# Per-tile waits on reused memory, and an adjacency proof that shares its stage with the next layer's prologue

## The chip, the cores and the metric

The kernel runs on one core of a Trainium2 chip. The metric is the time of one execution on the device in microseconds (us); three runs of the kernel before give a median of 2050.09 us. The engines are TensorE (PE, its weight loads PEld), VectorE (DVE), ScalarE (ACT), GpSimd (POOL) and SyncE (SP). SP and POOL here mostly issue transfers (DMA); "SPq" or "ACTq" in a view means that engine's queue of instructions.

## What is computed

Four graph layers run over 4096 nodes with 128 features and one dense adjacency matrix of 4096 x 4096 (f32, symmetric in the inputs, ones at about 1.6% of the places). Each layer's result is added to its input and normalised per row:

```python
x = _layernorm(x + _L0_gnn_ref(x, adj, ...))   # hyperbolic attention over pairs
x = _layernorm(x + _L1_gnn_ref(x, adj, ...))   # 4-head transformer attention
x = _layernorm(x + _L2_gnn_ref(x, adj, ...))   # normalised graph convolution
x = _layernorm(x + _L3_gnn_ref(x, adj, ...))   # additive attention, masked softmax
```

The part of layer 1 that the change touches is

```python
q = x @ Wq + bq;  k = x @ Wk + bk;  v = x @ Wv + bv        # 4 heads of 32
attn = einsum('nhc,mhc->hnm', q, k) / sqrt(32)
e = where(adj == 0, 0, exp(attn - rowmax));  out = (e / sum(e)) @ v
x_r = x @ Ws + bs                                            # gated with out
```

## The kernel before, in words

The adjacency is tiled in 8 x 8 blocks of 512 x 512. A class `Fast` computes everything under assumptions on the data (symmetric adjacency of zeros and ones, bounded scores) and proves them on the way; if a proof fails, a general class `Net` computes all again. With these inputs only `Fast` does work.

The program is written in a tile framework. Code opens pools (`tc.tile_pool`), which are laid out one above the other as a stack in SBUF or in the eight banks of PSUM, and takes tiles from them; a closed pool's memory is given to the next one. The framework inserts the semaphores. It also plans, at compile time, one fixed order of instructions for each engine, by priority (earlier code first) among what its own simulated clock says is ready; on the chip each engine works through its list in order. Inside `tc.manual_schedule()` the written order is kept, but other instructions can be placed between.

The stages, with times from the profile:

- **Layer 0** (0 to about 721 us). A short prologue, then `pair_loop` (L1709; to 646) over the 36 block pairs I <= J, in an order written out by hand (`SHARED_ORDER`). Its pools are `sg0`, `wk0` and PSUM pools `ps_z0`, `ps_i0`, `ps_j0`, all eight banks. Beside it POOL copies the adjacency as bf16 into the DRAM tensor `adjb` (`narrow`, L1917, last issued at 544). The end of layer 0 (L510 to L602 and `normalise_tile`) works on all 32 row tiles of X and finishes with ACT L232, in eight groups of four tiles.
- **The proof of symmetry**, `mirror` (L1664), is called at L513, between the pair loop and the end of layer 0. For each block pair SP loads `low` (L1683) and `up` (L1686), 512 KB each, into three buffers each (pool `mirt`); PE adds the block, weighted by -2^k, and the transposed mirror block, weighted by 2^k, into a PSUM bank (L1692, L1697; pool `mirp`, two banks); after twelve quarter blocks DVE takes the largest absolute value into a column of `odd` (L1702). There are 28 pairs, then 8 diagonal blocks: 64 loads, 144 quarter blocks, 12 reductions.
- **Layer 1's prologue**, in `layer1` (L2150), from the `with ExitStack() as pctx` on. PE transposes X into `XT` in eight groups (L163 in a helper; copies L178 on ACT, L180 on DVE). Then for each of eight column chunks and for k and q: a projection on PE (L2201), its rounded part by ACT (L2203) and its rest by DVE (L2204) into a tile `cut` (512 KB), a maximum by DVE (L2207), and a transfer to the DRAM tensor `qk` by SP (L2210). For the first two chunks POOL reads `qk` back as stacks of heads into `KS` and `QS` (`stack`, L2181, four transfers of 256 KB each time). Then V (PE L2216, DVE L2217) and the residual projection R (PE L2226, DVE L2227; R is the tile `Y` of later stages). All PSUM tiles of this stage come from the pool `ps_t`, eight banks, one bank each, in rotation. The last step is `good` (L2241).
- **Attention**, `attention_unshifted` (L1941), 789.9 to 1589.8: 256 steps of scores (PE L1994), exponential (ACT L2001), mask (DVE L2003) and weighted sum (PE L2020), two steps apart. `ps_s` takes six banks, `ps_v` two. Each output block has an `ending`.
- **Layers 2 and 3**, `layers23` (L2245): `Y` is split into three bf16 parts (`split`, ACT L2353, DVE L2355), PE convolves with blocks in a `ring` (L2372), and DVE looks at rows of the adjacency in tiles `nat` (loads L2331, L2336). Then `attend_factored` (L1573).

The pools that a stage opens wait, before their first use, for every earlier user of each pool on whose memory they lie.

Of the kernel before, what the change touches and what calls it, by code (L numbers as in the profile page):

```python
# [9 lines left out]
F32 = mybir.dt.float32  # L10
F32R = mybir.dt.float32r
# [6 lines left out]
P = 128  # L18
# [43 lines left out]
class Net:  # L62
# [30 lines left out]

    def copies(self):
        self.adjT = self.dram.tile([self.NS, self.NS, P, 4, S], F32, tag="adjT", name="adjT")

    def pools(self, ctx, adj, big, t, o):

        self.on_scalar = 4
        if adj:  # L100
            self.adjp = ctx.enter_context(self.tc.tile_pool(name="adjp", bufs=adj))
        if big:
            self.ps_big = ctx.enter_context(self.tc.tile_pool(name="ps_big", bufs=big, space=PSUM))
        self.ps_t = ctx.enter_context(self.tc.tile_pool(name="ps_t", bufs=t, space=PSUM))
        self.ps_o = ctx.enter_context(self.tc.tile_pool(name="ps_o", bufs=o, space=PSUM))
# [202 lines left out]
    def layer0(self, x, weight, bias, att_w, att_b):  # L308
# [4 lines left out]
        with ExitStack() as ctx:  # L313
            self.on_scalar = 4
            keep = ctx.enter_context(tc.tile_pool(name="keep0", bufs=1))
            self.cols = ctx.enter_context(tc.tile_pool(name="cols0", bufs=1))
            adp = ctx.enter_context(tc.tile_pool(name="ad0", bufs=2))
            pre_pools = ctx.enter_context(ExitStack())
            pre = pre_pools.enter_context(tc.tile_pool(name="pre0", bufs=2))
            self.ps_t = pre_pools.enter_context(tc.tile_pool(name="ps_t", bufs=6, space=PSUM))  # L320
            one = pre_pools.enter_context(tc.tile_pool(name="one0", bufs=1))
            self.wide = pre_pools.enter_context(tc.tile_pool(name="wide", bufs=1))
            ps_c = pre_pools.enter_context(tc.tile_pool(name="ps_c", bufs=1, space=PSUM))
# [187 lines left out]
            late = ctx.enter_context(tc.tile_pool(name="late0", bufs=1))  # L511
            rot = ctx.enter_context(tc.tile_pool(name="rot0", bufs=6))
# [92 lines left out]
    def pair_loop(self, HT, HA, dr, rows, adp, early, rows4):  # L605
# [7 lines left out]
        with ExitStack() as ctx:  # L613
            atp = ctx.enter_context(tc.tile_pool(name="at0", bufs=2))
            wtp = ctx.enter_context(tc.tile_pool(name="sg0", bufs=6))
            wk = ctx.enter_context(tc.tile_pool(name="wk0", bufs=2))
            ps_t = ctx.enter_context(tc.tile_pool(name="ps_t0", bufs=2, space=PSUM))
            ps_z = ctx.enter_context(tc.tile_pool(name="ps_z0", bufs=2, space=PSUM))
            ps_i = ctx.enter_context(tc.tile_pool(name="ps_i0", bufs=1, space=PSUM))
            ps_j = ctx.enter_context(tc.tile_pool(name="ps_j0", bufs=1, space=PSUM))  # L620
# [224 lines left out]
    def layer1(self, Wq, bq, Wk, bk, Wv, bv, Ws, bs, Wb, R):  # L845
# [6 lines left out]
        with ExitStack() as ctx:  # L852
            self.on_scalar = 4
            keep = ctx.enter_context(tc.tile_pool(name="keep1", bufs=1))
# [27 lines left out]
            with ExitStack() as pctx:  # L882
                pre = pctx.enter_context(tc.tile_pool(name="pre1", bufs=1))
                rot = pctx.enter_context(tc.tile_pool(name="rot1", bufs=2))
                self.ps_t = pctx.enter_context(tc.tile_pool(name="ps_t", bufs=8, space=PSUM))
# [59 lines left out]
    def attention_unshifted(self, VA, KS, QS, at0, stack, R, wb):  # L945
# [4 lines left out]
        with ExitStack() as ctx:  # L950
            rot = ctx.enter_context(tc.tile_pool(name="rotf", bufs=1))
            natp = ctx.enter_context(tc.tile_pool(name="natf", bufs=2))
            atp = ctx.enter_context(tc.tile_pool(name="atf", bufs=1))
            ep = ctx.enter_context(tc.tile_pool(name="ef", bufs=3))
            ps_s = ctx.enter_context(tc.tile_pool(name="ps_s", bufs=3, space=PSUM))
            ps_v = ctx.enter_context(tc.tile_pool(name="ps_v", bufs=1, space=PSUM))
# [198 lines left out]
    def attention_shifted(self, V, qk, R, wb, spare):  # L1155
# [4 lines left out]
        with ExitStack() as ctx:  # L1160
            self.pools(ctx, 1, 2, 3, 1)
            self.wide = ctx.enter_context(tc.tile_pool(name="wide", bufs=2))
            keep = ctx.enter_context(tc.tile_pool(name="keeps", bufs=1))
            self.cols = ctx.enter_context(tc.tile_pool(name="cols1", bufs=1))
# [12 lines left out]
            work = ctx.enter_context(tc.tile_pool(name="work1", bufs=1))  # L1177
# [98 lines left out]
    def layers23(self, w2, weight, bias, a_s, a_r, out, Y):  # L1276
# [6 lines left out]
        with ExitStack() as ctx:  # L1283
            RING = 8
            ring = ctx.enter_context(tc.tile_pool(name="ring", bufs=1)).tile([P, RING, 4, S], F32, tag="ring", name="ring")
            keep = ctx.enter_context(tc.tile_pool(name="keep3", bufs=1))
# [10 lines left out]
            pre = pctx.enter_context(tc.tile_pool(name="pre3", bufs=1))  # L1297
            rot = pctx.enter_context(tc.tile_pool(name="rot2", bufs=2))
            wp = pctx.enter_context(tc.tile_pool(name="w2", bufs=4))
            ps_b = pctx.enter_context(tc.tile_pool(name="ps_b", bufs=2, space=PSUM))  # L1300
            ps_t = pctx.enter_context(tc.tile_pool(name="ps_t", bufs=2, space=PSUM))
            ps_s = pctx.enter_context(tc.tile_pool(name="ps_s", bufs=2, space=PSUM))
            ps_a = pctx.enter_context(tc.tile_pool(name="ps_a", bufs=2, space=PSUM))
# [228 lines left out]
    def attend_factored(self, F, XB, rho, col, wx, tot, eps, a0, ring, out):  # L1532
        nc, tc, N, NT, NS, D, X = self.nc, self.tc, self.N, self.NT, self.NS, self.D, self.X
        with ExitStack() as ctx:
            rot = ctx.enter_context(tc.tile_pool(name="rot3", bufs=2))
            RING = ring.shape[1]
            wp = ctx.enter_context(tc.tile_pool(name="w3", bufs=4))
            ps_a = ctx.enter_context(tc.tile_pool(name="ps_a3", bufs=2, space=PSUM))
            ps_b = ctx.enter_context(tc.tile_pool(name="ps_b3", bufs=2, space=PSUM))
# [43 lines left out]
    def attend(self, H, Rb, ring, weight, br, a_s, a_r, out):  # L1583
        nc, tc, N, NT, D, X = self.nc, self.tc, self.N, self.NT, self.D, self.X
        with ExitStack() as ctx:
            self.pools(ctx, 0, 0, 6, 2)
            self.wide = ctx.enter_context(tc.tile_pool(name="wide", bufs=2))
            one = ctx.enter_context(tc.tile_pool(name="one3", bufs=1))
            self.cols = ctx.enter_context(tc.tile_pool(name="cols3", bufs=1))
# [4 lines left out]
            with tc.tile_pool(name="pre3", bufs=1) as pre:  # L1594
# [15 lines left out]
            work = ctx.enter_context(tc.tile_pool(name="work3", bufs=1))  # L1610
# [33 lines left out]
class Fast(Net):  # L1644

    MARKS = 112

# [16 lines left out]
    def mirror(self, ctx):  # L1664
# [3 lines left out]
        keep = ctx.enter_context(tc.tile_pool(name="mir", bufs=1))  # L1668
        rot = ctx.enter_context(tc.tile_pool(name="mirt", bufs=3))
        ps = ctx.enter_context(tc.tile_pool(name="mirp", bufs=2, space=PSUM))  # L1670
# [38 lines left out]
    def pair_loop(self, HT, HA, dr, rows, adp, early, rows4):  # L1709
# [7 lines left out]
        with ExitStack() as ctx:  # L1717
            wtp = ctx.enter_context(tc.tile_pool(name="sg0", bufs=6))
            wk = ctx.enter_context(tc.tile_pool(name="wk0", bufs=2))
            ps_z = ctx.enter_context(tc.tile_pool(name="ps_z0", bufs=4, space=PSUM))  # L1720
            ps_i = ctx.enter_context(tc.tile_pool(name="ps_i0", bufs=1, space=PSUM))
            ps_j = ctx.enter_context(tc.tile_pool(name="ps_j0", bufs=1, space=PSUM))
# [218 lines left out]
    def attention_unshifted(self, VA, KS, QS, at0, stack, R, wb):  # L1941
# [3 lines left out]
        W = C + 1  # L1945
        with ExitStack() as ctx:
            rot = ctx.enter_context(tc.tile_pool(name="rotf", bufs=1))
            natp = ctx.enter_context(tc.tile_pool(name="natf", bufs=2))
            atp = ctx.enter_context(tc.tile_pool(name="atf", bufs=1))
            ep = ctx.enter_context(tc.tile_pool(name="ef", bufs=3))  # L1950
            ps_s = ctx.enter_context(tc.tile_pool(name="ps_s", bufs=3, space=PSUM))
# [627 lines left out]
```

## Time and profile before

| what | value |
|---|---|
| median of three runs | 2050.09 us (2048.27 to 2053.14) |
| the profiled execution | 2050.21 us, span 2048.4 us, mean granted PE clock 0.954 |
| PE busy | 1900.9 us, 93% of the span |
| DVE busy | 1736.6 us, 85% |
| ACT busy | 1328.8 us, 65% |
| POOL busy | 171.4 us, 8% |
| moved by DMA | 350.22 MB, mean 171 GB/s |
| pair loop | about 76 to 646 us |
| end of layer 0 | 646 to 721 us |
| proof | first load 646.0, last reduction 744.8 us |
| layer 1's prologue | 745.7 to 789.8 us |
| attention | 789.9 to 1589.8 us |

A row of the page's groups names line, engine and operation, the tile written and those read, count, busy time and mean, and the idle time of the engine just before with what ended it. A row of the waits reads "who <- whom: us in total, times, longest us". A row of the chain gives start, length and what ran or was waited for; the chain is followed back from the last instruction. A row of the windows gives, for one stretch, the busy us of each engine with instruction counts in brackets, then the granted clock, the mean busy share of the DMA engines, and what they moved. Matmul ends are modelled, and DMA shares can come out above 1.

### The profile page before, as it was taken

How to read it: one execution, taken by the hardware profiler on the slowest of the kernel's cores; microseconds unless marked ns; L12 is line 12 of the kernel's file. 1: busy time of each engine (PE TensorE's matmuls, PEld its weight loads, DVE VectorE, ACT ScalarE, POOL GpSimd, SP SyncE). 2: the span in 40 equal slices, each digit the busy share in tenths (PEclk: the TensorE clock that was granted, in tenths of full speed). 3: DMA queues.
4: the chain of work that ended last, by engine and by line, in shares of the span. 5: the costliest groups of instructions: out<-in, count | busy, mean ns of one | idle time of the engine just before them, and what ended most of it. 6: DMA issues, size and time to landing. Idle time of an engine off the chain costs nothing.

```text
span 2048.4 us, 23818 instructions
## 1 busy us (share of the span) xinstructions
PE 1900.9 (93%) x8648; PEld 978.9 (48%) x8680; DVE 1736.6 (85%) x2685; ACT 1328.8 (65%) x1681; POOL 171.4 (8%) x269
## 2 busy tenths in 40 slices
PE   4789999999997788999999999999999799999997
PEld 4257766666666454333333333333333344444443
DVE  6579999998988946789999999999999777778986
ACT  5589999999997723777787777778787322210000
POOL 2211112111100221300000000000000000000000
PEclk8569999999999998999999999999999999999999
DMA  3488989899825977853535453545343799934441
GB/s 101 49 139 147 155 167 157 155 163 168 144 93 191 363 277 223 199 152 132 144 124 146 136 150 134 144 133 155 124 139 118 290 396 373 340 116 156 155 148 43
DMA packets 138064, 350.22 MB, mean 171 GB/s; under 512 B 13196, under 2 KB 56364, under 8 KB 125648
## 3 DMA queue, kind: packets, MB, share of 16 engines
q1 hardware_dynamic: 82944, 230.27, 32.3%
q0 software_dynamic: 45632, 50.69, 20.1%
q10 hardware_dynamic: 9360, 67.64, 9.9%
q8 instruction: 70, 1.15, 0.2%
q14 instruction: 58, 0.48, 0.1%
HBM read 371.54 MB, written 44.12 MB: 203 GB/s over the span
## 4 chain that ended last, share of the span: by engine, by line
PE 49%; DVE 24%; ACT 16%; DMA 6%; issue 4%; SPq 0%; POOL 0%; another core or an unknown queue 0%; ACTq 0%; DVEq 0%; POOLq 0%
PE pv L2020 11%; PE pa L1573 9%; DVE e L2003 9%; PE pa L2372 7%; PE ps L1994 6%; ACT e L2001 4%; PE pz L1775 3%; DMA up<-adjb 3%; DVE nat L1985 2%; ACT w L1792 2%; PE pi L1859 2%; PE pj L1874 2%; ACT s L1815 2%; ACT y L1811 2%; ACT y L1807 1%
## 5 line engine op out<-in xcount | busy, mean ns | idle before, releaser
L2003 DVE SCALAR_TENSOR_TENSOR e<-at,e 128x2048 f32<-128x2048 bf16 x256 | 582.6, 2286 | 77.3 <-ACT e L2001 76.7
L2001 ACT ACTIVATE e<-ps 128x1024 f32<-128x1024 f32 x512 | 492.9, 1024 | 150.6 <-PE ps L1994 121.6
L2020 PE MATMUL pv<-e,VA 128*64 128x512 f32 x2048 | 497.6, 607 | 6.7 <-DVE e L2003 5.7
L1994 PE MATMUL ps<-QS,KS 128*128 128x512 f32 x1024 | 314.8, 425 | 9.1 <-ACT e L2001 8.5
L1994 PEld LDWEIGHTS ps<-QS,KS 128*128 128x128 f32 x1024 | 170.9, 189 | 236.5 <-ACT e L2001 177.4
L2020 PEld LDWEIGHTS pv<-e,VA 128*64 128x64 f32 x2048 | 125.1, 136 | 250.2 <-issue 214.4
L1573 PE MATMUL pa<-w,Y 128*128 128x512 f32 x448 | 195.3, 594 | 0.0
L1775 PE MATMUL pz<-HT 128*128 128x512 f32 x288 | 171.8, 681 | 15.0 <-DVE w L1847 10.2
L1570 DVE SCALAR_TENSOR_TENSOR w<-rho,col,ring 128x512 f32<-128x512 f32 x224 | 162.7, 746 | 22.3 <-PE pa L1573 9.7
L2372 PE MATMUL pa<-ring,Y 128*128 128x512 bf16 x750 | 172.7, 384 | 8.7 <-ACT Y L2353 6.7
L1859 PE MATMUL pi<-HA,w 128*128 128x129 f32 x1152 | 156.6, 286 | 6.5 <-ACT s L1815 5.3
L1859 PEld LDWEIGHTS pi<-HA,w 128*128 128x128 f32 x1152 | 143.3, 199 | 18.2 <-issue 10.2
L1573 PEld LDWEIGHTS pa<-w,Y 128*128 128x128 f32 x448 | 83.8, 190 | 105.9 <-issue 80.3
L1976 ACT ACTIVATE nat<-nat 128x2048 f32<-128x2048 f32 x64 | 122.6, 1915 | 2.8 <-DMA nat<-in_adj_dram 2.8
L1874 PE MATMUL pj<-HA,w 128*128 128x129 f32 x896 | 120.7, 293 | 3.4 <-DVE X L1888 2.4
L2372 PEld LDWEIGHTS <-Y 128*128 128x128 bf16 x768 | 75.4, 99 | 100.9 <-ACT Y L2353 9.7
L1784 DVE TENSOR_SCALAR t<-pz 128x512 f32<-128x512 f32 x144 | 93.6, 682 | 30.2 <-PE pz L1778 30.2
L1874 PEld LDWEIGHTS pj<-HA,w 128*128 128x128 f32 x896 | 112.8, 205 | 11.2 <-issue 6.8
L1823 DVE SCALAR_TENSOR_TENSOR t<-t,s 128x2048 f32<-128x2048 f32 x36 | 82.3, 2286 | 13.4 <-ACT s L1815 13.4
L1792 ACT ACTIVATE w<-di,dr 128x512 f32<-128x512 f32 x144 | 90.6, 707 | 1.5 <-DMA di<-rows 1.5
L2336 DVE SCALAR_TENSOR_TENSOR nat<-nat 128x2048 f32<-128x2048 f32 x32 | 73.1, 2287 | 20.5 <-DMA nat<-in_adj_dram 20.5
L1847 DVE TENSOR_TENSOR w<-w,ptz 128x512 f32<-128x512 f32 x112 | 73.4, 681 | 18.7 <-PE ptz L1842 17.3
(410 smaller groups left out, 2343.1 us busy)
## 6 DMA issues: line engine op xcount, KB each, us to landing
nat<-in_adj_dram ACTq DMA_DIRECT2D x64, 1024.0 KB, 5.1
ring<-adjb SPq DMA_DIRECT2D x128, 512.0 KB, 4.7
ad<-in_adj_dram SPq DMA_DIRECT2D x36, 1024.0 KB, 9.4
adjb<-in_adj_dram POOLq DMA_DIRECT2D x64, 512.0 KB, 11.4
nat<-in_adj_dram SPq DMA_DIRECT2D x32, 1024.0 KB, 7.5
at<-adjb SPq DMA_DIRECT2D x63, 512.0 KB, 3.5
low<-adjb SPq DMA_DIRECT2D x36, 512.0 KB, 5.1
up<-adjb SPq DMA_DIRECT2D x28, 512.0 KB, 6.6
```

The costliest lines, as they stand in the source:

```text
L1570: nc.vector.scalar_tensor_tensor(w, rho[:, I * S : (I + 1) * S], col[:, 0, j : j + 1], at[:, jb, :], op0=ALU.max, op1=ALU.mult)
L1573: nc.tensor.matmul(pa, lhsT=F[:, j, :], rhs=w, start=False, stop=(j == NT - 1), skip_group_check=True)
L1775: nc.tensor.matmul(pz, lhsT=HT[:, j * P : (j + 1) * P], rhs=HT[:, I * S : (I + 1) * S], start=True, stop=False)
L1792: nc.scalar.activation(w[:, jb, :], st[p]["d"][k], AF.Sigmoid, bias=dr[:, 4 * J + jb : 4 * J + jb + 1])
L1859: nc.tensor.matmul(row[I, "po"][ib // 2][:, ib % 2, :], lhsT=st[p]["w0"][:, jb, ib * P : (ib + 1) * P], rhs=HA[:, 4 * J + jb, :], start=False,
L1874: nc.tensor.matmul(pj[:, a, :], lhsT=st[p]["w1"][:, ib, jb * P : (jb + 1) * P], rhs=HA[:, 4 * I + ib, :], start=(ib == 0), stop=(ib == 3),)
L1976: nc.scalar.activation(nat, nat, AF.Identity, accum_out=self.deg2[:, k, i : i + 1])
L1994: nc.tensor.matmul(p[:, h, :], lhsT=KS[:, h2 + h, jb * P : (jb + 1) * P], rhs=QS[I % 2][:, h2 + h, :], start=True, stop=True,)
L2001: nc.scalar.activation(e[:, h2 : h2 + 2, :], p, AF.Exp)
L2003: nc.vector.scalar_tensor_tensor(e, at[:, jb % 4, :].unsqueeze(1).to_broadcast([P, NH, S]), 0.0, e, op0=ALU.not_equal, op1=ALU.mult,)
L2020: nc.tensor.matmul(st["po"][h // 2][g : g + 64, :], lhsT=VA[:, o : o + 64], rhs=e[:, h, :], start=(jb == 0), stop=(jb == NT - 1), skip_gro ...
L2372: nc.tensor.matmul(st["pa"], lhsT=parts[k][:, j, :], rhs=at[:, jb, :], start=(I > 0 and j == k == 0), stop=(j == NT - 1 and k == 2), skip_ ...
```

## The change

There are three parts.

1. Every pool is opened by a new method `pool`, which passes `reuse_waits`. For `Fast` it is `"tile"`: a tile waits for the users of the tiles whose memory it takes, not for all users of the pools there. For `Net` it stays `"pool"`.
2. The proof's three pools are allocated from the other end of the memory (`side="right"`) and put on a stack of contexts of their own, `self.proof`, which is closed at the end of layer 1's prologue and not at the end of layer 0. To make room, `ps_t` in the prologue has six banks instead of eight, and `cut` five buffers instead of seven.
3. `mirror` notes the priority at its start (`self.rank`). The prologue runs under `tc.high_priority` with an offset that puts its instructions just before that rank: in planning, on every engine, they come ahead of the proof's.

No instruction of the computation is added or removed.

```diff
+    waits = "pool"
+
+    def pool(self, **kw):
+        return self.tc.tile_pool(reuse_waits=self.waits, **kw)
...
 class Fast(Net):
     MARKS = 112
+    waits = "tile"
...
     def mirror(self, ctx):
-        keep = ctx.enter_context(tc.tile_pool(name="mir", bufs=1))
-        rot = ctx.enter_context(tc.tile_pool(name="mirt", bufs=3))
-        ps = ctx.enter_context(tc.tile_pool(name="mirp", bufs=2, space=PSUM))
+        self.proof, self.rank = ExitStack(), tc.cur_priority
+        keep = self.proof.enter_context(self.pool(name="mir", bufs=1, side="right"))
+        rot = self.proof.enter_context(self.pool(name="mirt", bufs=3, side="right"))
+        ps = self.proof.enter_context(self.pool(name="mirp", bufs=2, space=PSUM, side="right"))
...
             with ExitStack() as pctx:
-                pre = pctx.enter_context(tc.tile_pool(name="pre1", bufs=1))
-                rot = pctx.enter_context(tc.tile_pool(name="rot1", bufs=2))
-                self.ps_t = pctx.enter_context(tc.tile_pool(name="ps_t", bufs=8, space=PSUM))
+                pctx.enter_context(self.proof)
+                pctx.enter_context(tc.high_priority(tc.cur_priority - self.rank + 1))
+                pre = pctx.enter_context(self.pool(name="pre1", bufs=1))
+                rot = pctx.enter_context(self.pool(name="rot1", bufs=2))
+                self.ps_t = pctx.enter_context(self.pool(name="ps_t", bufs=6, space=PSUM))
...
-                        cut = rot.tile([P, 2, S], F32R, tag="cut", name="cut", bufs=7)
+                        cut = rot.tile([P, 2, S], F32R, tag="cut", name="cut", bufs=5)
```

Every other line of the diff replaces `tc.tile_pool(` by `self.pool(`.

## The prediction

> **What bounds the kernel now.** I read the slices of the page first. Counted from 0, slices 12 to 15 stand out: TensorE drops from 9 to 7 or 8 tenths while the transfers peak.
>
> ```profile
> PE   4789999999997788999999999999999799999997
> ...
> GB/s 101 49 139 147 155 167 157 155 163 168 144 93 191 363 277 223 199 152 132 144 124 146 136 150 134 144 133 155 124 139 118 290 396 373 340 116 156 155 148 43
> ```
>
> A slice is 51.2 us, so this is 614 to 819 us. I cut that stretch at the places where the timelines change character. Columns after the time: busy us and instructions of PE, PE weight loads, DVE, ACT, POOL; then granted clock, DMA share, GB/s.
>
> ```profile
> 646.00:720.00 74.00, 50.57 (x471) 32.90 (x481) 65.68 (x355) 56.95 (x248) 15.58 (x24) 0.93 0.96 360
> 720.00:745.00 25.00, 17.75 (x193) 12.80 (x197) 2.32 (x5) 0.81 (x3) 0.00 (x1) 1.00 0.78 281
> 745.00:762.00 17.00, 16.33 (x62) 9.27 (x63) 14.03 (x23) 8.92 (x14) 8.57 (x10) 1.00 0.65 211
> 762.00:776.00 14.00, 10.46 (x59) 8.94 (x57) 8.20 (x13) 3.99 (x6) 5.43 (x10) 0.77 1.15 382
> 776.00:790.00 14.00, 11.87 (x77) 11.34 (x77) 11.99 (x22) 0.14 (x1) 0.54 (x1) 0.75 1.09 374
> ```
>
> From 646 to 720 the end of layer 0 (DVE 66 of 74 us) and the proof (DMA 0.96) run side by side. From 720 to 745 only the proof runs: DVE and ACT are 9% and 3% busy. Then layer 1's prologue takes 45 us, DMA-bound in its second half. The chain of waits says what starts the prologue and what stops it midway:
>
> ```profile
> 744.84 0.70 DVE odd L1702
> 745.67 3.69 PE pt L163 x32
> ...
> 761.76 13.58 DMA qk<-cut
> 775.45 0.70 ACT cut L2203
> ...
> 779.05 9.14 PE pt L2226 x64
> 788.22 0.69 DVE Y L2227
> ```
>
> The first transpose of the prologue (L163) waits for the proof's last reduction, though its input was ready by 721 (the last ACT X L232 starts at 719.16). `ps_t` takes all eight PSUM banks, and two are the proof's. After the prologue, attention is TensorE-bound (24.6 to 25.0 of every 25 us busy from 840 to 1515), so an earlier start moves the end by the same amount. The waits of the DMA queue and of the engines in this stretch:
>
> ```profile
> SPq L1683 <- PE pm L1697: 55.6, 29, 4.3
> SPq L1683 <- DVE w L1836: 14.4, 1, 14.4
> ...
> SPq L1683 <- PE pi L1859: 5.9, 1, 5.9
> ...
> ACT cut L2203 <- DMA qk<-cut: 13.3, 6, 3.3
> ```
>
> **Removed: the prologue's wait for the proof.** Between X ready (721) and the first transpose (745.7) lie 24.7 us. Were nothing else late, attention's first score matmul would move from 789.9 to 765. That is the ceiling of this edit, but the bytes do not vanish. The proof loads 36 `low` and 28 `up` of 512 KB, 33.6 MB; the prologue writes 16 `qk` of 512 KB, 8.4 MB, and reads back 16 stacks of 256 KB, 4.2 MB; with `at0` 46.7 MB. At the 360 to 382 GB/s of the rows above (I take 370) that is 126 us of DMA. Before, they spread over 646 to 790 with a hole from 725 to 760. Without the hole, starting at 646, all would be done at 772.
>
> **Moved: the start of the proof.** Its first load waits until 646 for the whole of the pair loop's pools (the two SP rows above). By tile and from the right-hand end its 30 KB per partition lie on the last tags of `wk0`, which ends the stack of the pair loop: by the tags' sizes and first uses `er` 4, `dj` 6, `s` 8 KB and one `y` of 8 (an estimate from the code). Their last readers end between 610 and 635; the last `adjb` writes are out at 544 on POOL. So loads can start near 632. Six buffers (3.1 MB, 8 us) fit ahead of the first matmul, which still needs the two banks of `pj` (free at 641.6; the first proof matmul now starts at 649.7). Bounds: 0 (the queue places them no earlier) to 10 us of DMA; I take 5, so all bytes are through near 767. The end of layer 0 may likewise start its 64 dot products before the last block: DVE idles 4.4 us there (641.6 to 646.0), a gain of 0 to 4 that counts only where DMA is not the limit; I take none.
>
> **The prologue under contention.** Transposes can follow X group by group from 705, the first `qk` write near 708. DVE has, from 698, the end of layer 0 (21 us to 719), 2.5 for XT, 16 x (0.746 + 0.677) = 22.8 for cut and maximum, 8 x 0.68 twice = 10.9 for V and R, 5 reductions of 0.69: about 61 us, so 759 if it never waits. It does wait, for `cut`: five buffers instead of seven, and with seven ACT already waited 13.3 us. The Trainium skill ("DMA: Bandwidth & Descriptors", Issuing engines are not separate DMA queues) says that DMAs from any engine share the same 16 DMA engines and interleave; so priority on the engines is none in the rings. The row gives a `qk` write a median 12.9 us to land with up to seven out. By the rule, a write now stands with up to six proof loads and four writes, 5.2 MB, 14 us at 370 GB/s: five buffers give 16/5 x 14 = 45 us, the last cut near 708 + 45 = 753. By the row alone (priority as if it held in the rings; 5 x 0.52 MB at 370 GB/s, 7 us) it would be 16/5 x 7 = 22, and DVE's 744 decides. I take the rule, 753.
>
> Behind the last cut, in allocation order, come the rest of V and all of R: 13.7 us before (776.2 to 789.9). With six banks two more tiles are left behind it, 2 x 1.15 us of PE (9.14 us for 8 tiles); the wait for `good` before the first score falls (0.4 to 2 us). Sum 14 to 15, so scores start near 768 instead of 789.9: 22 us. The first `pv` came 8.9 us later (two table loads of 1.28, the first exponentials and masks). It needs the proof's two banks, free near 767 + 3, so before 768 + 9: no new wait, but only 7 us of slack.
>
> Who stands behind whom: on SP a proof load waits for PE to free its buffer and holds up a `qk` write; on PE a proof matmul waits for its load and holds up prologue matmuls; on DVE a reduction waits for PE (23.6 us over six times now) with cuts behind it; on POOL `VA`'s memset waited 54 us for the proof and now goes early, ahead of the stacks. In the trace before, seven of twelve reductions stand between DVE's instructions of layer 0's end and their stalls are under 1 us until 719: the planned order meets the real transfer rate, so I price order stalls at 0 to 10 us and take 0 beyond the shared rings.
>
> **Other pools by tile.** The pair loop's first distance matmul (75.9) follows the last prologue bank: 0 to 2 us, I take 0. At the end of attention, layer 2's first `nat` loads issue at 1605.6, behind the output block's last use of the old pool, and DVE waits 4.07 us for them with the splits behind it, on which PE waits (4.42 us at 1614.5). Their tiles lie mostly on `at0`, `ev` and `o`, free from 1591 to 1603: 4 us gained, bounds 0 and 6. Ring loads keep their place (small loads onto `VA` ahead of them need the last `pv`). More waits per instruction have no row here; nothing between 0 and 2 us, I take 0.
>
> **Sum.** 22 + 4 = 26. The profiled execution took 2050.21 us (span 2048.4); its time is 0.1 us above the median 2050.09, so it carries over: 2024.
>
> **A second rule.** "TensorE: Matmul & The Clock Gate" (Why this matters for your kernels) says gaps over about 3 us drop the clock to half. The rows show granted 0.77 and 0.75 from 762 to 790, with PE gaps of 0.5 to 1.7 us. By the rule interleaved proof matmuls fill gaps and R's 9.14 us could be 8; by the row, half clock could come from more short stalls, +3. I take 0.
>
> **Rivals.**
> (a) Shared rings, as summed: 2024, own range 2014 to 2034. Chance 0.58.
> (b) The prologue wins the rings: last cut at 744, scores at 758, proof done 767, pv with little delay: 30 + 4 + 3 from earlier starts, 2013. For it: writes wait for nothing once cut. Against: one SP queue for both. 0.17.
> (c) It does not do what it says: the planned order puts most proof matmuls and loads ahead of the prologue's; the transposes still come near 738. Only the earlier proof (5) and the nat loads (4) remain: 2041. For it: in-order queues, priorities act only in planning. Against: the reductions' places above. 0.14.
> (d) Slower: five `cut` buffers with queue-blocked writes. If a `qk` write needs over 21.6 us from cut to free, 16/5 x 21.6 = 69 us puts the last cut past 777 and eats the whole gain; at 26 us (double of 12.9) the last cut is at 791, scores 15 us late, less 4: 2061. In favour: the shared queue and 13.3 us of such waits with seven; against: 370 GB/s would have to fall to about 240. 0.07.
> (e) Losses just cancel: 2050, 0.04.
>
> **How the numbers follow.** About 0.2% (4 us) is what a measurement of this kernel can tell from no change. Faster: a, b, c and nothing of d, e: 0.89; same 0.04; slower 0.07. The range takes a, most of b and c: 2008 to 2042.
>
> **What would show it.** Right: L163 before the last L1702, near 705 to 725; first L1994 near 768, first L2020 within 10 us behind it; DMA at 340 GB/s or more through 720 to 765; `qk` landing 12 to 16 us. Wrong: L163 after 738 (c), landing over 20 us (d), `pv` waiting for L1702 by more than a few us, or attention itself longer than its present 800 us.

## The result and the profile after

The changed kernel takes 2033.55 us (median of 7, 2024.85 to 2040.42) beside 2048.27 us before (median of 7 on the same chip): ratio 0.9922, 95% interval 0.9898 to 0.9946. Run a second time, unchanged, it gave 2029.06 us, 0.9906 (0.9888 to 0.9924). Forecast was 2024; the gain is 15 to 19 us instead of 26. Its profiled execution took 2031.6 us, span 2029.8.

The slices of its page, beside those of before: slice 14 (717 to 768 us before; 710 to 761 here, where a slice is 50.7 us) now moves 360 GB/s in place of 277, and slice 15 178 in place of 223, so the stage is denser and ends earlier; but slice 13 moves 335 in place of 363. Line numbers from here on are those of the changed kernel, 5 to 9 above those of before: L168 was L163 (transposes), L1690 and L1693 were L1683 and L1686 (loads of the proof), L1699, L1704 and L1709 were L1692, L1697 and L1702 (its products and reductions), L2210 and L2225 were L2201 and L2216 (projections, V), L2001, L2010 and L2027 were L1994, L2003 and L2020 (scores, masks, `pv`).

```profile
PE   4679999999998688999999999999999899999997
...
GB/s 101 61 137 150 176 141 170 155 159 159 151 79 226 335 360 178 197 146 131 158 126 152 128 147 134 155 132 138 127 143 114 324 396 368 333 111 156 154 150 44
```

The same stretch of the changed kernel, cut where its character changes (columns as before: busy us of PE, PE weight loads, DVE, ACT, POOL; granted clock, DMA share, GB/s):

```profile
640.00:650.00 10.00, 8.48 (x86) 6.69 (x86) 8.30 (x64) 5.61 (x39) 0.00 (x0) 1.00 0.43 143
650.00:690.00 40.00, 28.43 (x275) 18.50 (x280) 33.72 (x147) 35.18 (x162) 20.13 (x25) 0.96 0.98 373
690.00:720.00 30.00, 21.49 (x176) 14.35 (x180) 25.82 (x138) 17.27 (x46) 0.00 (x0) 0.89 0.73 274
720.00:752.00 32.00, 24.64 (x133) 15.18 (x133) 21.57 (x34) 11.42 (x17) 10.93 (x20) 1.00 1.09 368
752.00:770.00 18.00, 14.15 (x112) 12.01 (x114) 10.04 (x20) 0.00 (x0) 0.00 (x0) 0.81 1.07 395
770.00:786.00 16.00, 12.70 (x121) 9.12 (x123) 4.50 (x5) 7.62 (x8) 0.00 (x0) 1.00 0.51 179
```

The one hole of before (725 to 760) is gone, and three smaller ones stand in its place: 640 to 650, 690 to 720 and 770 to 786. At 385 GB/s (an estimate of full rate, from the 373 and 395 above) they lack 2.4, 3.3 and 3.3 MB, together 23 us of transfers. The third is in part the end of the work, since the last load of the proof lands at 781.5; counted up to there (249 GB/s from 770) it lacks 1.6 MB, and the sum is 19 us. The chain shows the second and the third from TensorE's side:

```profile
697.80 0.50 ACT X L237
698.35 0.86 PE pt L168 x2
...
719.05 0.88 PE pqk L2210 x2
...
736.75 13.53 DMA qk<-cut
750.39 0.70 ACT cut L2212
...
753.38 15.07 DMA low<-adjb
771.93 1.20 PE ps L2001 x5
774.61 4.13 DMA low<-adjb
783.49 2.29 DVE e L2010
785.92 1.94 PE pv L2027 x8
```

The first transposes (L168) now wait for X and no longer for the proof. But where before's chain went from the last cut through V and R straight to the scores, it now goes back to the proof: `low` at 753.38 and once more at 774.61. TensorE's waits in this stage (640 to 800) say the same, and the last row, of SP's queue from 690 to 720, gives the hole there:

```profile
PE pm L1704 <- DMA up<-adjb: 12.8, 16, 2.3
PE pt L168 <- ACT X L237: 7.7, 4, 6.3
PE pt L2225 <- DVE cut L2213: 7.3, 6, 1.7
PE pm L1699 <- DMA low<-adjb: 5.5, 5, 2.8
...
SPq L1690 <- PE pm L1704: 15.1, 4, 9.7
```

While TensorE stood for 6.3 us at a transpose, it ran no product of the proof and freed none of its buffers, and SP, whose next load needs one, waited up to 9.7 us and issued nothing from 692.1 to 702.2.

The order in which the planner put the work stands behind both. On SP: 27 pairs of proof loads, all 16 writes of `qk`, then the last 10 proof loads (one pair, 8 diagonal blocks). On TensorE: 361 of the proof's 678 products, then the transposes among the products, all eight groups of them ahead of all but one projection, and behind the product for `good` still 122 proof products before the first `pv`.

**One warning about reading two profiles.** In this execution the pair loop ended 3.1 us earlier than before's. It can't be credited to the change: in the experiments a kernel with the same instructions in the same order on every engine up to there (the writes on ScalarE, below) ended it 6.2 us later than this one, and over all executions of kernels with waits by tile the end lies between 633.3 and 644.3, with before's 641.2 inside. So every mark from here on is counted from the last addition of `pj` to X (641.2 before, 638.1 after; start of the instruction):

| mark, us from the last addition of pj | before | after | after, again | waits by tile only | no proof |
|---|---|---|---|---|---|
| first proof load | 4.8 | -10.2 | -10.9 | 0.0 | (one load) |
| last reduction of the proof | 103.6 | 144.8 | 147.1 | 99.5 | (6.4) |
| first cut on ACT | 109.1 | 81.8 | 82.6 | 103.9 | 82.8 |
| last cut on ACT | 134.3 | 112.3 | 113.0 | 128.5 | 115.8 |
| last R product | 146.7 | 122.3 | 123.0 | 140.6 | 126.1 |
| first score | 148.7 | 132.2 | 132.5 | 142.4 | 127.9 |
| first pv | 157.6 | 147.8 | 150.1 | 149.9 | 135.0 |
| last pv | 948.0 | 934.9 | 937.0 | 938.6 | 924.1 |
| last pv to last product of layer 2's convolution (L2381; L2372 before) | 199.8 | 197.3 | 197.1 | 197.2 | 197.7 |

Down to the last `pv` the changed kernel gains 13.1 us (11.0 in its second execution), and in layer 2 another 2.5 (2.7): 13.7 to 15.6 by the marks, 15 to 19 by the medians. What the medians show beyond the marks would lie in layer 0, and a rival for it was not tested. The granted clock of the whole execution varies, and the time goes with it: of the changed kernel's seven executions the two at 0.956 and 0.957 took 2036.9 and 2040.4 us, the five at 0.963 to 0.966 2024.9 to 2034.1. Its median clock is 0.964, that of waits by tile alone 0.963, that of the kernel with waits by pool (experiment 2) 0.957, that of before 0.955 to 0.958 in the three sets on record. Whether waits by tile raise the clock, and how much of the medians that is, stays open; the marks behind the pair loop do not contain layer 0.

### The profile page after: what moved, and what is told of

The parts are those of the page before. It is cut to its first block, busy times and chain, and to the rows that moved or that the text cites. A ratio compares the mean times of both kernels' runs of the same rounds, so it can differ in the third digit from the quotient of the medians.

```text
span 2029.8 us, 23817 instructions
## 1 busy us (share of the span) xinstructions
PE 1884.2 (93%) x8647; PEld 973.1 (48%) x8680; DVE 1738.2 (86%) x2685; ACT 1328.8 (65%) x1681; POOL 172.6 (9%) x269
## 4 chain that ended last, share of the span: by engine, by line
PE 47%; DVE 27%; ACT 17%; issue 4%; DMA 4%; SPq 0%; POOL 0%; ACTq 0%; DVEq 0%; POOLq 0%
PE pv L2027 11%; PE pa L1578 10%; DVE e L2010 9%; PE pa L2381 7%; PE ps L2001 6%; ACT e L2008 4%; DVE nat L1992 2%; ACT w L1799 2%; PE pj L1881 2%; PE pi L1866 2%; PE pz L1782 2%; DVE t L1830 2%; ACT s L1822 2%; ACT y L1818 2%; ACT nat L1983 1%
## 5 line engine op out<-in xcount | busy, mean ns | idle before, releaser
L2010 DVE SCALAR_TENSOR_TENSOR e<-at,e 128x2048 f32<-128x2048 bf16 x256 | 582.7, 2286 | 67.4 <-ACT e L2008 66.9
L2027 PE MATMUL pv<-e,VA 128*64 128x512 f32 x2048 | 495.8, 605 | 7.4 <-DVE e L2010 7.4
L2001 PE MATMUL ps<-QS,KS 128*128 128x512 f32 x1024 | 313.2, 424 | 4.1 <-ACT e L2008 3.7
L2001 PEld LDWEIGHTS ps<-QS,KS 128*128 128x128 f32 x1024 | 170.3, 188 | 229.3 <-ACT e L2008 173.7
L2027 PEld LDWEIGHTS pv<-e,VA 128*64 128x64 f32 x2048 | 124.7, 136 | 250.2 <-issue 214.3
L2381 PE MATMUL pa<-ring,Y 128*128 128x512 bf16 x750 | 172.3, 383 | 6.6 <-ACT Y L2362 4.5
L1782 PE MATMUL pz<-HT 128*128 128x512 f32 x288 | 160.9, 641 | 17.4 <-DVE w L1854 8.0
L2381 PEld LDWEIGHTS <-Y 128*128 128x128 bf16 x768 | 75.6, 99 | 98.4 <-issue 8.6
```

Source lines behind the costliest of these rows:

```text
L1782: nc.tensor.matmul(pz, lhsT=HT[:, j * P : (j + 1) * P], rhs=HT[:, I * S : (I + 1) * S], start=True, stop=False)
L2001: nc.tensor.matmul(p[:, h, :], lhsT=KS[:, h2 + h, jb * P : (jb + 1) * P], rhs=QS[I % 2][:, h2 + h, :], start=True, stop=True,)
L2010: nc.vector.scalar_tensor_tensor(e, at[:, jb % 4, :].unsqueeze(1).to_broadcast([P, NH, S]), 0.0, e, op0=ALU.not_equal, op1=ALU.mult,)
L2027: nc.tensor.matmul(st["po"][h // 2][g : g + 64, :], lhsT=VA[:, o : o + 64], rhs=e[:, h, :], start=(jb == 0), stop=(jb == NT - 1), skip_gro ...
L2381: nc.tensor.matmul(st["pa"], lhsT=parts[k][:, j, :], rhs=at[:, jb, :], start=(I > 0 and j == k == 0), stop=(j == NT - 1 and k == 2), skip_ ...
```

## The experiments

Each is the changed kernel with one edit; times are medians beside the kernel before on the same chip. Single executions scatter by about 0.5% (28 of before: 2039.86 to 2058.9), so for the mechanism the marks count more than the medians. The marks of a kernel come from one profiled execution; the two of the changed kernel differ by up to 2.3 us.

**1. Waits by tile only.** Proof pools on the left and closed with layer 0, as before.

```
-        self.proof, self.rank = ExitStack(), tc.cur_priority
+        self.proof = ctx                      # mir, mirt, mirp without side="right"
-                pctx.enter_context(self.proof)
-                pctx.enter_context(tc.high_priority(tc.cur_priority - self.rank + 1))
-   ps_t bufs=6, cut bufs=5
+   ps_t bufs=8, cut bufs=7
```

> The change with only its waits by tile: the proof's pools stand on the left and close with layer 0 as before, 8 banks and 7 cut buffers, no priority. Theory (the changed kernel's 18.6 us of span are four sums: 3.0 at the pair loop's start, 9.9 from the proof's overlap up to the first pv, 3.3 in the attention, 2.6 at layer 2's start; the first, the fourth and perhaps the third come from waits by tile): last X add of the pair loop near 643 (646.0 before), first pv near 796 (798.8), median 2039 to 2043. Rival A (everything comes from the overlap): 2047 to 2051, marks as before. Rival B (waits by tile alone let the prologue start beside the proof, too): first transpose before 740, median under 2036.

Measured: 2037.46 us, ratio 0.9951 (0.9929 to 0.9972). The marks are in the table: the proof starts 4.8 us earlier and ends 4.1 earlier, the prologue from first cut to first `pv` takes 46.0 us in place of 48.5, layer 2 gains 2.6. The first theory missed: it had this kernel's first `pv` near 796, and it came at 787.7. So this part of the change alone brings more than half of the gain, and the kept memory with its priority adds 1.6 to 3.7 us at the last `pv` (medians: 4 to 8 us, taken on different chips; this interval overlaps that of the changed kernel's first set and just misses that of its second). The rival that the overlap brings everything fell too. What is left of the old hole here shows how much the overlap could have filled:

```profile
690.00:720.00 30.00, 20.91 (x201) 13.88 (x202) 24.42 (x137) 17.43 (x45) 0.00 (x0) 0.94 0.97 359
720.00:750.00 30.00, 24.87 (x191) 16.70 (x192) 12.08 (x20) 8.80 (x14) 7.00 (x8) 1.00 0.60 199
750.00:780.00 30.00, 24.38 (x141) 20.51 (x139) 23.21 (x38) 4.25 (x7) 7.55 (x14) 0.83 1.14 382
```

From 720 to 750 only 199 of about 385 GB/s move: 5.6 MB, 14.5 us. That, and not 24.7 us, is what keeping the memory had to offer behind the waits by tile.

**2. Waits by pool, the rest of the change kept** (`waits = "pool"` in `Fast`).

> The changed kernel with waits by pool everywhere; proof kept, priority, 6 banks and 5 cut buffers stay. Theory: the overlap keeps its 9.9 us, the pair loop's start (3.0) and layer 2's start (2.6) go back to before: first pv near 789, median 2035 to 2040. Rival A (all from the overlap): 2032 to 2034. Rival B (with waits by pool the prologue's pools wait for the whole of layer 0's, so that the overlap is lost as well): first transpose after 718, median 2044 to 2051.

Measured: 2042.22 us, 0.9962 (0.9945 to 0.9980). First load -1.1, first cut +81.6, first `pv` +153.1, last `pv` +942.0, last `pv` to last L2381 199.9. As the theory had it, layer 2's 2.5 us need the waits by tile (199.9 here, 196.8 to 198.8 in all twelve with them); the first `pv` was 5 us later than it said, and the median lies between its range and that of rival B. The overlap starts without them (first cut as after), and brings 4.5 us at the first `pv` and 6.0 at the last; its profiled execution, of 2049.2 us, was one of the two longest of its fourteen.

**3. No priority** (the line with `high_priority` taken out). SP's order becomes 58 loads, then the last 6 between the first three writes; the proof's products stand ahead of V and R.

> The changed kernel without the one line that gives the prologue priority. Theory (what the changed kernel lacks is the end of the proof: its last 10 loads stand behind all 16 writes of the cuts on SP, and 122 of its products stand ahead of the first pv on TensorE): without priority the planner puts the last 8 loads before and between the first three writes and the proof's products ahead of V and R; loads run without the hole at 690 to 710, the proof ends near 735 to 750, the first pv comes at 768 to 778, median 2016 to 2026. Rival A (priority is what brings the overlap): first transpose after 735, median 2038 to 2048. Rival B (the bytes alone set the first pv): first pv 783 to 789, median 2031 to 2035.

Measured: 2038.47 us, 0.9953 (0.9932 to 0.9974). The proof did end early (last reduction +114.3), but the last cut moved from +112.3 to +133.7 and the first `pv` to +153.1. The theory that the loss lies in the ten loads behind the writes fell: with them ahead, the writes pay. The rival's time was right for another reason, since the transposes did start early (first cut +80.2). Without priority the kept memory is worth nothing over waits by tile alone (0.9951).

**4. The writes on ScalarE's queue**, so that no proof load stands behind a write.

```
-                        nc.sync.dma_start(out=qk[a, :, :, s]...
+                        nc.scalar.dma_start(out=qk[a, :, :, s]...
```

> The changed kernel with the 16 writes of the cuts issued by ScalarE's queue in place of SP's. Theory: no proof load stands behind a write any more; the loads run on through 717 to 752, the last reduction of the proof comes before 775 and the first pv with it, median 2020 to 2027. Rival A (bytes alone set the end): first pv 783 to 789, median 2031 to 2035. Rival B (ScalarE now waits at each write for VectorE's half of the cut, and its next cut stands behind that): cuts end after 765, no gain or slower, 2033 to 2045.

Measured: 2032.21 us, 0.9914 (0.9889 to 0.9938), the changed kernel's time. Loads and writes now run side by side; the 16 writes take 44.0 us to issue (+83.9 to +127.9) in place of 30.5, the last reduction comes at +148.0, the first `pv` at +151.1. The theory fell, with the last reduction not before but behind the changed kernel's; the bytes' rival named the median. The loads did not run on although no write stood before them: after the 54th they left in ones and twos up to +137.6, and SP waited for products of the proof (L1704 and L1699) by up to 14.0 us.

**5. Transposes later.** The prologue's transposes use an identity to which a mark of the proof (zero) has been added, so that the planner must put them behind that reduction: behind 541 products for the ninth mark, behind 639 for the eleventh (`self.odd[:, 10:11]`).

```
-                self.transposed(X, XT)
+                paced = pre.tile([P, P], F32, tag="paced", name="paced")
+                nc.vector.tensor_scalar(paced, self.ident, self.odd[:, 8:9], None, op0=ALU.add)
...
+                        nc.tensor.transpose(p[:, k, :], X[:, t, :], paced)
```

> The changed kernel with one added dependency: the prologue's 64 transposes use a copy of the identity to which the proof's ninth mark (zero here) has been added, so that the planner puts them behind 541 of the proof's 678 products in place of 361, and SP's order becomes 58 proof loads, the 16 writes, 6 loads of 4 MB in place of 54, 16, 10. Times from the last addition of pj to X. Theory (the changed kernel loses its time where TensorE stands at its first transposes waiting for X, 6.3 us, and runs at a lower clock behind that, which stops the proof's loads; the proof ends late, and the first pv stands behind 122 of its products): no wait of over 2 us for X, DMA over 340 GB/s in every stretch between +50 and +80, the proof's last reduction near +125 (+144.8 in the changed kernel), first pv at +132 to +138 (+147.8), median 2018 to 2025. Rival A (the bytes set it): last reduction after +140, first pv +145 to +150, median 2031 to 2036. Rival B (the start of the transposes sets it, and they now start some 14 us later): writes of the cuts end after +122, first pv after +148, 2034 to 2042.

> The same with the writes of the cuts on ScalarE's queue, so that all 64 proof loads follow each other on SP. Theory: as with the writes on SP up to +75; the last loads issue by +85, the proof ends before +110, the writes end near +118, first pv +130 to +137, median 2016 to 2024. Rival A (bytes): first pv +145 to +150, 2031 to 2036. Rival B (cuts stand in ScalarE's queue behind their writes): last cut after +125, first pv +140 to +150.

> As the first of this group, but with the eleventh mark: the transposes stand behind 639 of 678 products, and all 64 loads before the first write. Tells the wait for X from the place of the last loads: no transposes wait for X, nothing of the proof is left behind the writes, but the prologue starts only when the proof is nearly over. Theory: DMA without a hole, loads end near +80, transposes +82 to +95, cuts +92 to +120, first pv +138 to +144, median 2023 to 2031. Rival B (an early start of the prologue is what the changed kernel gains by): first pv as with waits by tile alone (+150), median 2036 to 2040. Rival A (bytes): +145 to +150.

| | median us | ratio | last reduction | last cut | first pv | last pv |
|---|---|---|---|---|---|---|
| ninth mark | 2030.05 | 0.9904 (0.9877 to 0.9930) | +146.2 | +119.0 | +149.3 | +936.7 |
| ninth, writes on ACT | 2035.07 | 0.9937 (0.9918 to 0.9955) | +140.9 | +130.9 | +148.4 | +937.5 |
| eleventh mark | 2041.12 | 0.9954 (0.9935 to 0.9974) | +142.7 | +131.9 | +151.7 | +941.3 |

The wait for X is gone in all three, and nothing came of it. The windows of the first (ninth mark) show why:

```profile
640.00:650.00 10.00, 10.00 (x97) 8.14 (x96) 8.15 (x67) 3.60 (x25) 0.00 (x0) 1.00 0.24 82
...
690.00:710.00 20.00, 14.59 (x137) 9.54 (x136) 19.65 (x106) 10.63 (x27) 1.87 (x1) 0.91 0.97 363
710.00:740.00 30.00, 24.83 (x146) 14.77 (x144) 19.47 (x55) 14.14 (x30) 4.52 (x9) 0.94 0.77 266
740.00:770.00 30.00, 24.53 (x167) 20.75 (x165) 19.43 (x31) 4.81 (x7) 6.37 (x12) 0.83 1.13 387
770.00:790.00 20.00, 13.92 (x115) 9.52 (x115) 6.11 (x11) 8.29 (x8) 0.00 (x0) 0.91 0.51 192
```

690 to 710 is full now, and the hole of 690 to 720 stands at 710 to 740. There SP issues nothing in two stretches: from 711.5 to 720.0, for which the trace names no clear cause, and from 721.5 to 729.8, where the next transfer in its order is the first write, which waits for TensorE's 32 transposes (from 723.8) and the first cut behind them. From 723.8 to 738.4 TensorE runs these and 13 projections in one block and frees no slot of the proof. The second theory, the stall at the transposes, fell as well. The eleventh mark comes out nearly like waits by tile alone, as its rival B said.

**6. The proof left out**, all but its last block (63 of 64 loads and 667 of 678 products; the verdict on symmetry then rests on that block).

> The changed kernel with all of the proof left out but its last block (1 load of 64, 11 of 678 products; the verdict on symmetry then rests on that block alone). It gives the prologue's own limit. Theory: X is ready at +80, no proof stands anywhere; cuts +82 to +105, first pv +118 to +125 in place of +147.8, the end of the kernel 23 to 30 us before the changed kernel's, 2004 to 2010. Rival (the prologue's own chain of writes, buffers and products is the limit in the changed kernel, and the proof costs little): first pv +140 or later, median over 2022.

Measured: 2019.88 us, 0.9853 (0.9831 to 0.9875). First `pv` +135.0, 10 to 17 us later than expected: the prologue has a floor of its own. Its chain:

```profile
719.88 1.20 PE pqk L2210 x2
721.10 0.69 ACT cut L2212
...
726.35 9.00 DMA qk<-cut
...
736.96 12.55 DMA qk<-cut
...
764.43 0.71 PE ps L2001 x2
...
771.54 3.53 PE pv L2027 x8
```

With nothing else on the rings the cuts still take 33 us (+82.8 to +115.8) behind their own writes and stacks, 12.6 MB in all, at 365 to 381 GB/s from 730 to 750; the first `pv` follows the first cut by 52 us. One thing is not equal: without the proof TensorE is idle before the transposes, and its granted clock was 0.50 from 650 to 720 and 0.76 from 719 to 752 (1.00 from 720 to 752 in the changed kernel), so the floor may be a little lower than this run shows.

**7. Half of the products, half of the loads, fewer slots.**

```
half of the products:  for each block pair only jb 0 and 1 are multiplied; all loads kept
half of the loads:     up = low, 28 loads of 64 left out; marks go to a tile that nobody reads
two slots:             mirt bufs=3 -> bufs=2
```

> The changed kernel with half of the proof's products left out (the third and fourth of each pair of blocks' four groups), all its loads kept, so that the verdict on symmetry rests on half of the entries: the same bytes, half of TensorE's work for the proof. Times from the last addition of pj to X; +147.8 in the changed kernel, +135.0 without the proof. Theory now (neither an order alone nor the bytes: the proof's products and the prologue's stand in one order on TensorE, each wait in it stops the others, and the proof's three pairs of slots are too few to keep the DMA engines going meanwhile): first pv +137 to +142, DMA without a hole under 300 GB/s between +20 and +130, median 2022 to 2028. Rival (bytes alone): first pv +146 to +150, median 2030 to 2036.

> The changed kernel with 28 of the proof's 64 loads left out (the mirrored block is not loaded, the products read the first block in its place, and the reductions go to a tile that nobody reads, so nothing is proven): 14.7 MB less, all of TensorE's work kept. The planner puts 588 of the proof's products ahead of the first transpose here. Bytes alone: first pv +135 to +138, median 2019 to 2025. TensorE's order and work: with the products never short of loads, the proof is done by +75 to +85, and the prologue then runs as it does with no proof: first pv +135 to +140. If TensorE's work alone were the limit: first pv +145 or later, median over 2030.

> The changed kernel with two pairs of slots for the proof's blocks in place of three. Theory (slots couple the DMA engines to TensorE's order): the holes in the transfers grow, last reduction of the proof +152 to +165, first pv +153 to +168, median 2038 to 2052. Rival (bytes alone): within 2 us of the changed kernel, 2030 to 2036.

| | median us | ratio | last reduction | first cut | first pv | last pv |
|---|---|---|---|---|---|---|
| half of the products | 2031.36 | 0.9920 (0.9901 to 0.9938) | +142.5 | +81.1 | +145.5 | +931.9 |
| half of the loads | 2026.52 | 0.9882 (0.9861 to 0.9902) | +79.7 | +92.0 | +142.0 | +931.4 |
| two pairs of slots | 2057.35 | 1.0040 (1.0022 to 1.0058) | +173.1 | +96.4 | +176.1 | +960.7 |

Leaving out half of TensorE's products for the proof brings 2.3 us at the first `pv`, and my expectation missed; the numbers are the rival's. The hole from 690 to 720 is still there (252 GB/s), with TensorE waiting 8.6 us at a transpose for X. So the amount of work is hardly the limit; but the test is not a clean one, since TensorE, less busy, had a granted clock of 0.59 in place of 0.96 from 650 to 690 and did each product more slowly (569 ns in place of 396 for L1699, 297 in place of 226 for L1704). Taking 14.7 MB away (38 us at 385 GB/s) brings 5.8: here 588 products are planned ahead of the transposes, the last X is ready 9 us later (+90.4 against +81.2) and with it the first cut 10 us later, and the prologue's own 50 us follow. So this run does not measure the bytes cleanly; the bytes' forecast (+135 to +138) missed, and so did mine (+135 to +140), by 2. Two slots in place of three cost 26 to 28 us at the first `pv`, and the kernel is slower than before the change. The clean part of this answer is the stretch from 650 to 690, where TensorE does nothing but products of the proof and SP nothing but its loads: 298 GB/s against 373. The rest has more than one cause, for X too is ready 13.5 us later (+94.7), and the planner now leaves 13 loads behind the writes in place of 10. The windows of that kernel, against 373 GB/s and 274 GB/s in the changed kernel's same stretches:

```profile
650.00:690.00 40.00, 22.79 (x213) 13.61 (x211) 31.54 (x138) 32.21 (x155) 16.36 (x25) 0.94 0.83 298
690.00:720.00 30.00, 20.82 (x177) 13.80 (x176) 24.09 (x114) 11.95 (x28) 3.58 (x1) 0.91 0.71 260
...
770.00:814.00 44.00, 28.93 (x237) 21.33 (x237) 11.81 (x20) 8.03 (x8) 0.00 (x0) 0.88 0.59 218
```

**8. The changed kernel again.**

> The changed kernel once more, unchanged. If the 3 us by which its profiled execution was ahead at the end of the pair loop belong to the execution and not to the change, the last addition of pj to X stands anywhere from 636 to 645 here and the stretches behind it as before: first pv +146 to +150, last pv +933 to +937, median 2030 to 2036, ratio 0.990 to 0.994. If the change brings them: 637 to 639.

Measured: see the table of marks; 2029.06 us. The last addition of `pj` started at 637.5, which by itself fits both readings; the kernel with its writes on ScalarE, identical up to there, had it at 644.3, so single profiles cannot show a gain of 3 us there.

**What the runs say together.** From the first cut to the first `pv` the prologue takes 48.5 us alone (before) and 66.0 us beside the proof (after). The overlap brings the first cut forward by 27.3 us and gives back 17.5. In every order tried with the whole proof and three pairs of slots, the first `pv` lay between +147.8 and +153.1. Whoever goes last pays: with the writes first the proof ends at +145 to +148, with the loads first or beside them the last cut comes at +126 to +134. What the two whose windows stand above share are rings (the DMA engines and their queues) that lack 19 to 22 us of transfers up to the proof's last load (estimates from the windows of the changed kernel and of the ninth mark). A proof load leaves only when its turn on SP has come and TensorE, in its fixed order, has freed one of three pairs of slots. SP's wait of 9.7 us shows this for the hole from 690 to 720, and two slots show it in one direction. The other, a fourth pair (8 KB more per partition), was not tried; so it stays open whether more slots would close the holes, and the rival that the bytes alone set the end, which named the median of several runs, is weakened by the holes but not excluded. Taken singly, waits by tile bring 10 us (ratio 0.9951) and the overlap with waits by pool 8 (0.9962), together 16 to 19: about the sum. No version with the whole proof beats the changed kernel beyond the intervals; with the proof free of cost it would end 9 to 14 us earlier (2019.88).

## Why the prediction was right or wrong

**Direction right, mechanism in part.** The first transpose came at 698, ahead of the proof's last reduction, and followed X. The loads started at 627.9 (forecast 632). Attention began earlier and the end moved with it; layer 2's loads gained too. But the forecast had the first score 22 us earlier because the prologue runs beside the proof. Waits by tile alone, with no prologue beside the proof, already bring 6.3 us at the first score and 9.4 at the last `pv`; the overlap adds only 1.6 to 3.7 us at the last `pv` (4 to 8 by the medians). That the time lies as near to the forecast as it does is in part luck.

**The step that failed: "all bytes are through near 767", with order stalls at 0.** The sum took 370 GB/s from the first load on, without a hole, and so put the proof's banks as free at 770 and "no new wait" behind the first score. Measured, the last reduction came at +144.8, against +128.8 in the forecast (770 less 641.2), and the rings lacked about 19 us of full rate up to the last load. The range of 0 to 10 us for such stalls was too short, and the reason for taking 0 (reductions between DVE's instructions stalled under 1 us until 719) spoke of a stretch in which the planner had nothing but proof for TensorE and SP. A fixed order there says nothing of one with a second customer in it.

**Where the 22 us went.** The first score moved 16.5 us (148.7 to 132.2), 5.5 short. The last cut was on the spot (+112.3, forecast 753, that is +111.8), and the R products ended at +122.3. But the product for `good` stood behind proof products that waited for the loads behind the writes: from R to the first score 9.9 us, against 2.0 before and 1.8 without a proof. From the first score to the first `pv` it took 15.6 us instead of 8.9: most of the 122 products stand between them on TensorE, and DVE's first mask (L2010, 783.49) is queued behind three reductions, the last at 782.88. That gives back 6.7 more, and the first `pv` gained 9.8 (7.5 in the second execution) of 22. The sign by which the prediction wanted to be proved wrong, "`pv` waiting for L1702 by more than a few us", is there, though not by the path that the prediction had in mind (the proof's two banks): `pv` waits for the mask, and the mask for the reduction. From there to the last `pv` 3.3 of it return; why is not shown (12 score products stand before the first `pv` in every kernel, so the scores had not run further ahead). Had the forecast been compared with a kernel without a proof, the error would have shown: its first `pv` (777, +135.8) is that of experiment 6 (+135.0), where the proof costs nothing.

**The rule on the rings.** The last cut was right through two errors that cancel. The first write left at 721.4 instead of 708, since all transposes are planned ahead of the projections. And the 16 writes took 30.5 us instead of 45: the planner put all of them in one block on SP, so that from 717.3 to 752.3 no new load was issued, and a write landed in a median 10.4 us, not 14. So here priority did hold in the rings, but only because it decided what SP issued. With loads and writes issued from two queues (experiments 4 and 5) they interleave, as the Trainium skill, "DMA: Bandwidth & Descriptors" (Issuing engines are not separate DMA queues) has it, and the 16 writes took 44.0 and 44.4 us. That this is near the forecast's 45 does not confirm its working: a write landed in a median 11.8 and 7.9 us there, not 14, and the writes left in groups with pauses of 11 to 15 us between them.

**The clock.** I took 0. The wait of 6.3 us at the transposes came with a granted clock of 0.75 from 690 to 700 (1.00 to 695, then 0.50) and 0.91 in the ten us behind; the transposes took 322 ns in place of 274, 1.5 us over 32. The Trainium skill's "TensorE: Matmul & The Clock Gate" (Why this matters for your kernels), which says that a gap of more than about 3 us drops the clock to half, agrees with this one wait, at a small price here. The three later-transposes kernels avoid the wait and gain nothing measurable.

**Layer 2's start:** 4 forecast, 2.5 and 2.7 measured, within its bounds of 0 to 6. **The pair loop:** 0 forecast; the 3.1 us in the profile lie within what executions differ by. **Earlier loads by tile:** 5 forecast, 4.8 by waits by tile alone. **Rivals:** (c), no overlap, was near in time for the kernel with waits by tile only (2037 against 2041) but not in mechanism; (d), slower through buffers, did not come true for `cut` (last cut in time with five), and did for one pair of proof slots less.

## What to carry to other kernels

When two streams of work are to overlap, first measure each alone (leave one out): the floor is the slower one's own chain, and the gain is the idle transfer time left between them, not the length of the wait that falls. If a stream's loads depend on buffers that another in-order engine frees, count how many microseconds of transfers its slots cover, and look for a hole wherever that engine does something else for longer. And try the smallest part of a change by itself: here waits by tile, without any overlap, brought more than half. Leaving work out changes more than that work: here it changed the planner's order and the granted clock too, so look at both before the time is read.

## What the runs showed of the hardware

- Loads of 512 KB with two pairs of slots moved 298 GB/s (650 to 690 us), with three pairs 373 in the changed kernel, and 350 to 389 in the eight other profiles with the whole proof and three pairs (one of them the changed kernel again); this is slots and TensorE's order together, not the rings alone.
- The same program starts in two ways: in eight profiled executions the first `pi` product came at 107.0 to 108.6 us, in the six others at 118.2 to 118.8. In all executions of the first kind the granted clock from 70 to 110 us was 0.76, in all of the second 0.50. The pair loop's end does not follow it closely (633.3 to 642.2 and 636.7 to 644.6 us). One profile per kernel cannot tell 3 us in layer 0.
